# A graph layer with edge sums, a linear-attention mix and a 30-step feed-forward: W's products of two groups placed in the chain to the mix, and two VectorE pieces of the first stage placed earlier

## The chip, the cores and the metric

The kernel runs on one core of one Trainium2 chip. The metric is the device time of one execution in microseconds (us); the time before is 4202.76 us, the median of 4 runs (4201.67 to 4215.41). A profile is one further execution, with its own time. In the profile PE is TensorE's matmul, PEld its weight load, DVE is VectorE, ACT is ScalarE, POOL is GpSimd and SP is SyncE, which here issues DMAs.

## The reference

`x` has 12500 nodes of 256 features; there are 200000 edges (`src`, `dst`, `edge_weight`), sorted by `dst`. All is float32.

```python
xn = layernorm(x)
agg = segment_sum((xn @ W)[src] * edge_weight[:, None], dst)           # edges
q, k, v = (split_heads(xn @ w.T) for w in (wq, wk, wv))                # 4 heads of 64
k, v = layernorm(k) * gk + bk, layernorm(v) * gv + bv                  # per head
kv = einsum('sd,se->de', k, v) / N                                     # per head
x = x + relu(agg) + concat_heads(q @ kv) @ wo.T + bo
h = layernorm(x)
for _ in range(30):
    h = h + 0.01 * tanh(h); h = silu(h); h = layernorm(h) * lw + lb; h = h @ Wf.T + b
x = x + h
```

## The kernel before, in words

Nodes stand in 98 tiles of 128, in 25 groups of four tiles (the last has two). Instructions are issued in an order that is written out by hand (`manual_schedule`), and each engine runs its own in that order.

**First stage** (the loop at L574, one group of `x` per turn). `x` is loaded (L89), its statistics are taken on DVE (`stats_of_x`, L506 and L508) and raised to the power -1/2 on POOL (L510, L512), DVE makes the shift (L519), ACT normalizes (L529), SP stores the rows to `xnd` in DRAM (L91), PE transposes them (L541) and ACT copies them to `xnT` (L547). The edge lists (`dst`, `src`, `edge_weight`) are turned to columns beside that (L374 to L422). `wkv`, the matrix of keys and values, is centred over its rows at L491 to L497 and over each head at L607 to L611 (`hm`), the latter in turn g == 2. From g == 3 on each turn also makes the keys and values of one tile.

**Keys and values.** For each tile t PE multiplies `xnT` by `wkv` (L288), ACT squares (L295), DVE sums (L299), ACT takes the root (L301), DVE inverts and scales (L305, L306), and two tiles later PE adds the product of keys and values to `pacc` (L314, `kv_product`). The tiles from 24 on run in the loop at L793.

**Edges.** 128 edges are one gather: POOL issues an indirect DMA (L182) of 128 rows of `xnd` into one of 16 buffers `xg`. Four gathers are a quad and two quads an octet. DVE builds selection matrices (L208, L213, L221), PE multiplies a quad's rows by them (`sum_quad`, L234), ACT copies an octet's sum (`copy_quads`, L245), and PE adds it to a window of nodes in PSUM (`add_quads`, L259). When no later octet touches 64 nodes, ACT copies them to `aT`, the group's transposed sums, and DVE clears them (`free_nodes`, L273 and L274). A gather is issued only when the quad that used its buffer before has been summed: at most 16 gathers stand ahead of the sums (`gathers`, L179). In the loop at L793 `octet_at` says after which tiles an octet is summed; they are tiles 30, 33, 37, ..., 86, 90, 93 and 97.

**The chain to the mix** (L823 to L863). From `pacc` on, each product needs the one before: `psum_kv` (L824), times `lk` (L829), copied to `y` (L832), times `rv` (L836), scaled to the block-diagonal `bd` (L839), times `wq` (L847), copied and centred over rows (L849 to L852), times `wo` (L856), plus the bias to `mix` (L861). Between these stand five calls of `another_quad` (L830, L833, L840, L848, L860): what is due of an earlier octet, one quad's sum, four gathers. `p_kv`, three PSUM buffers, holds the products.

**Steps** (`plan`, L872, and the loop at L1024). A step is a "mix" of one group (`xnT` times `mix`, plus `x`, L1076), a "W" of one group (`aT` times `wg`, plus the rows of `accw`, which are zeros unless an edge fell outside the windows, then relu, added to `base`, L1080 and L1081), or one "pass" of the 30-step loop for one group: transposes (L998), copies (L1005), product (L1011), tanh (L957), DVE (L963), silu (L964), statistics (L970), power on POOL (L976), scaling (L984). All these products stand at L1011. `plan` lists the steps beforehand from assumed costs (3.5 us a matrix, 4.4 a pass, 1.25 a gather, a pass of the same group 14.0 later), with how many quads and gathers go with each step; it takes all gathers issued so far as landed. A group's passes start when its "mix" and "W" are done, and at most five groups are active.

Of the kernel before, what the change touches and what calls it, by code (L numbers as in the profile page):

```python
# [8 lines left out]
F32 = mybir.dt.float32  # L9
# [21 lines left out]
def gps_layer(  # L31
# [135 lines left out]
    class Edges:  # L167
# [4 lines left out]
        freed = 0  # L172
        xg, sel, selq, sq, aT = {}, {}, {}, {}, {}
# [147 lines left out]
    with ExitStack() as ph:  # L321
# [167 lines left out]


        for i, name in enumerate(("k", "v")):  # L491
            nat = w_nat[name]
            cm = small.tile([P, KC], F32, name="cm")
            nc.vector.tensor_reduce(cm, nat, AX.X, ALU.add)
            nc.vector.tensor_scalar(cm, cm, 1.0 / C, None, ALU.mult)
            nc.vector.tensor_tensor(nat, nat, cm[:, :, None].to_broadcast([P, KC, C]), ALU.subtract)
            nc.scalar.copy(wkv[:, :, i * C : (i + 1) * C], transposes_of(nat))  # L497

# [69 lines left out]


# [4 lines left out]
        for g in range(NG + 2):  # L574
# [10 lines left out]
            if g < NG:  # L585
                stats_of_x(g)
            if 0 <= g - 2 < NL:
                list_stored(g - 2)
# [17 lines left out]
            if g == 2:  # L606
                wh = wkv.rearrange("p k (h d) -> p (k h) d", d=D)  # L607
                hm = small.tile([P, KC * 2 * HEADS], F32, name="hm")
                nc.vector.tensor_reduce(hm, wh, AX.X, ALU.add)
                nc.vector.tensor_scalar(hm, hm, 1.0 / D, None, ALU.mult)  # L610
                nc.vector.tensor_tensor(wh, wh, hm[:, :, None].to_broadcast([P, KC * 2 * HEADS, D]), ALU.subtract)  # L611
# [101 lines left out]
    with ExitStack() as ph:  # L713
# [16 lines left out]
        gcol = w1.tile([D, 2], F32, name="gcol")  # L730
        wo_nat = w1.tile([P, KC, C], F32, name="wo_nat")
# [55 lines left out]
        for t in range(kv_done, NT + 2):  # L787
            octet_at[t] = spent > 12.5 + 10.3 * n
            n += octet_at[t]
            spent += 2.3 + (2.2 if octet_at[t] else 0.0)  # L790
# [23 lines left out]
        def another_quad():  # L814
            copy_quads()
            free_nodes()
            selections(1)
            add_quads()
            sum_quad()
            gathers(Q)  # L820


# [3 lines left out]
        nc.vector.memset(bd, 0.0)  # L826
        py = p_kv.tile([D + 1, HEADS, P], F32, name="pkv")
        for hd in range(HEADS):
            nc.tensor.matmul(py[:, hd, :], lhsT=psum_kv[:, hd, :], rhs=lk[:, hd % (P // D), :], start=True, stop=True)  # L829
        another_quad()  # L830
        y = w1.tile([D + 1, HEADS, P], F32, name="y")
        nc.vector.tensor_copy(y, py)  # L832
        another_quad()  # L833
        pbd = p_kv.tile([P, HEADS, D], F32, name="pkv")
        for hd in range(HEADS):
            nc.tensor.matmul(pbd[:, hd, :], lhsT=y[:, hd, :], rhs=rv, start=True, stop=True)  # L836
        for hd in range(HEADS):
            r = slice(hd % (P // D) * D, (hd % (P // D) + 1) * D)
            nc.vector.tensor_scalar(bd[r, hd // (P // D), r], pbd[r, hd, :], 1.0 / N, None, ALU.mult)  # L839
        another_quad()  # L840


# [5 lines left out]
        another_quad()  # L848
# [3 lines left out]
        nc.vector.tensor_tensor(at, at, am[:, :, None].to_broadcast([P, KC, C]), ALU.subtract)  # L852
        pm = p_kv.tile([P, KC, C], F32, name="pkv")
# [6 lines left out]
        another_quad()  # L860
# [11 lines left out]
    def plan():  # L872
# [151 lines left out]
    for k in range(K + 3):  # L1024
# [150 lines left out]
```

## Time and profile before

| | us |
|---|---|
| median of 4 runs | 4202.76 |
| the profiled execution | 4214.08 |
| its span | 4212.3 |
| PE busy / PEld busy | 4072.4 / 3388.9 |
| DVE / ACT / POOL busy | 3400.7 / 2526.8 / 2575.3 |
| first stage, tiles 24 to 97 | 0 to 124, 124 to 396 |
| chain to the mix, until `mix` is there | 397.7 to 424.2 |
| first "mix" step's product, first "pass" step's product | 425.65, 483.92 |
| last gather's slice, then passes alone | about 3500, to 4212.3 |

The profile's page gives busy times and the span in 40 slices; its timeline gives every instruction's start, duration, shape and, in brackets, the idle time before it and what ended that; a table by stretches gives busy time and the clock that PE was granted (1.00 is full). Matmuls of float32 are recorded as two each. Starts of matmuls are measured and their ends modelled.

### The profile page before, as it was taken

To read this page: it belongs to the slowest core of one execution; us is meant where nothing else is said; L and a number is where in the kernel's file an instruction comes from. 1 tells how busy PE (TensorE), PEld (TensorE's weight loads), DVE (VectorE), ACT (ScalarE), POOL (GpSimd) and SP (SyncE) were. 2 spreads that over 40 slices of the span, in tenths; PEclk is the share of its full clock that TensorE was granted. 3 is DMA by queue.
4 is the path that set the end of the run, shared out by engine and by line. 5 is a ranking of instruction groups with operands and counts; after the bars stand their busy time and mean duration, and the time that the engine had idled before them with its cause. 6 is when DMAs were issued, how large, how long until landed. Compare 5 with 4: busy or idle time off the path is not lost.

```text
span 4212.3 us, 68082 instructions
## 1 busy us (share of the span) xinstructions
PE 4072.4 (97%) x24201; PEld 3388.9 (80%) x24201; DVE 3400.7 (81%) x7389; ACT 2526.8 (60%) x3762; POOL 2575.3 (61%) x3186
## 2 busy tenths in 40 slices
PE   8797899999999999999999999999999999999999
PEld 4454678888888888888788888887888888788888
DVE  8454568888888888888888888888888888888887
ACT  7332245666665666666666666656666666677776
POOL 3466667777767777777677777666666662222222
PEclk9898999999999999999999999999999999999999
DMA  8333422222222222222222222122221210000000
GB/s 259 93 88 88 150 87 66 64 67 62 64 64 78 81 61 70 70 64 63 79 75 70 70 64 74 58 80 71 67 66 57 66 51 9 21 1 1 1 1 23
DMA packets 147687, 278.36 MB, mean 66 GB/s; under 512 B 28047, under 2 KB 97197, under 8 KB 147341
## 3 DMA queue, kind: packets, MB, share of 16 engines
q0 software_dynamic: 75024, 204.97, 16.5%
q1 hardware_dynamic: 72173, 68.42, 5.2%
q8 instruction: 197, 3.23, 0.3%
q14 instruction: 149, 1.22, 0.1%
q10 hardware_dynamic: 144, 0.52, 0.0%
HBM read 247.68 MB, written 26.12 MB: 65 GB/s over the span
## 4 chain that ended last, share of the span: by engine, by line
PE 79%; DVE 12%; ACT 4%; issue 3%; another core or an unknown queue 1%; POOL 1%; DMA 0%; DVEq 0%; POOLq 0%; ACTq 0%
PE po L1011 54%; PE pt L998 14%; PE pq L234 4%; PE pa L259 3%; DVE z L984 3%; PE pkv L288 2%; DVE st L970 2%; DVE s L963 2%; ACT s L957 2%; DVE v L299 1%; PE pacc L314 1%; DVE x_st L506 1%; POOL rs L976 1%; DVE f_st L1131 0%
## 5 line engine op out<-in xcount | busy, mean ns | idle before, releaser
L1011 PE MATMUL po<-w,zT 128*128 128x256 f32 x11760 | 2669.8, 380 | 4.5 <-DVE big L1070 2.1
L1011 PEld LDWEIGHTS po<-w,zT 128*128 128x128 f32 x11760 | 2178.8, 190 | 282.2 <-issue 11.1
L182 POOL DMA_INDIRECT xg<-xnd,src_i x1563 | 1596.1, 1021 | 505.2 <-issue 341.5
L963 DVE SCALAR_TENSOR_TENSOR s<-s,po 128x1024 f32<-128x1024 f32 (+1 forms) x725 | 864.9, 1193 | 356.6 <-ACT s L957 306.8
L984 DVE TENSOR_SCALAR z<-s,st,rs 128x256 f32<-128x256 f32 x2940 | 1042.6, 418 | 68.8 <-POOL rs L976 66.4
L964 ACT ACTIVATE s<-s 128x1024 f32<-128x1024 f32 (+1 forms) x750 | 780.5, 1041 | 489.7 <-DVE s L963 478.5
L970 DVE BATCH_NORM_STATS2 st<-s 128x6 f32<-128x512 f32 x1470 | 937.7, 679 | 115.6 <-ACT s L964 100.4
L957 ACT ACTIVATE s<-po 128x1024 f32<-128x1024 f32 (+1 forms) x725 | 730.2, 1007 | 243.9 <-PE po L1011 224.0
L1005 ACT ACTIVATE zT<-pt 128x512 f32<-128x512 f32 x1470 | 801.0, 602 | 65.8 <-PE pt L998 59.4
L998 PE MATMUL pt<-ident,z 128*128 128x128 f32 x5880 | 789.0, 276 | 36.4 <-DVE z L984 34.8
L998 PEld LDWEIGHTS pt<-ident,z 128*128 128x128 f32 x5880 | 671.9, 142 | 170.1 <-issue 76.4
L976 POOL TENSOR_TENSOR rs<-ve,mhalf 128x4 f32<-128x4 f32 (+1 forms) x750 | 764.7, 1020 | 62.5
L974 POOL TENSOR_SCALAR ve<-st 128x4 f32<-128x4 f32 (+1 forms) x750 | 146.3, 195 | 977.8 <-DVE st L970 938.1
L245 ACT COPY sq<-pq 128x256 f32<-128x256 f32 x196 | 72.3, 369 | 354.4 <-PE pq L234 248.4
L234 PE MATMUL pq<-xg,sel 128*32 128x256 f32 x3126 | 219.2, 388 | 4.6 <-issue 3.5
L259 PE MATMUL pa<-selq,sq 128*128 128x192 f32 (+2 forms) x1168 | 186.7, 297 | 35.7 <-ACT sq L245 19.8
L259 PEld LDWEIGHTS pa<-selq,sq 128*128 128x128 f32 x1168 | 173.1, 195 | 48.0 <-ACT sq L245 21.7
L288 PE MATMUL pkv<-wkv,big 128*128 128x512 f32 x392 | 202.3, 639 | 9.7 <-DVEq L622 4.8
L273 ACT COPY aT<-pa 128x128 f32<-128x128 f32 x196 | 51.4, 262 | 216.9 <-PE pa L259 151.6
L234 PEld LDWEIGHTS pq<-xg,sel 128*32 128x32 f32 x3126 | 83.7, 109 | 103.9 <-issue 68.2
L299 DVE TENSOR_REDUCE v<-sq 128x8 f32<-128x512 f32 x98 | 66.7, 681 | 104.7 <-ACT sq L295 91.7
L288 PEld LDWEIGHTS pkv<-wkv,big 128*128 128x128 f32 x392 | 71.2, 200 | 69.8 <-issue 60.0
(150 smaller groups left out, 1534.7 us busy)
## 6 DMA issues: line engine op xcount, KB each, us to landing
xg<-xnd,src_i POOLq DMA_INDIRECT x1563
xt<-in_x_dram SPq DMA_DIRECT2D x48, 512.0 KB
xnd<-xt SPq DMA_DIRECT2D x24, 512.0 KB
xt<-accw SPq DMA_DIRECT2D x24, 512.0 KB
out_dram<-big SPq DMA_DIRECT2D x24, 512.0 KB
xg<-in_dst_dram SPq DMA_DIRECT2D x6, 128.0 KB
xg<-in_src_dram SPq DMA_DIRECT2D x6, 128.0 KB
xg<-in_edge_weight_dram SPq DMA_DIRECT2D x6, 128.0 KB
```

The costliest lines, as they stand in the source:

```text
L182: nc.gpsimd.indirect_dma_start(out=ed.xg[t], out_offset=None, in_=xnd, in_offset=bass.IndirectOffsetOnAxis(ap=src_i[:, t : t + 1], axis=0),)
L234: nc.tensor.matmul(ed.pq[j * 2 * WIN : (j + 1) * 2 * WIN, :], lhsT=sel[:, j, :], rhs=ed.xg.pop(q * Q + j), start=(q % 2 == 0), stop=last, ...
L259: nc.tensor.matmul(pa[:, k, c : c + hi - lo], lhsT=sq[:rows, k * P : (k + 1) * P], rhs=selq[:rows, lo - n0 : hi - n0], start=False, stop=( ...
L957: nc.scalar.activation(flat(s, nt), flat(h, nt), AF.Tanh)
L963: nc.vector.scalar_tensor_tensor(sf, sf, 0.01, flat(h, nt), op0=ALU.mult, op1=ALU.add)
L964: nc.scalar.activation(sf, sf, AF.Silu)
L970: nc.vector.bn_stats(st[:, q, :], s[:, q].rearrange("p c j -> p (c j)"))
L976: nc.gpsimd.tensor_tensor(rs[:, :nt], ve[:, :nt], mhalf[:, :nt], ALU.pow)
L984: nc.vector.tensor_scalar(z[:, j, :], s[:, j // 2, :, j % 2], sv[:, j, 1:2], rs[:, j : j + 1], ALU.subtract, ALU.mult)
L998: nc.tensor.transpose(pt[:, i, k, :], z[:, 2 * q + i, k * P : (k + 1) * P], ident)
L1005: nc.scalar.activation(zT[:, 2 * q : 2 * q + 2], pt, AF.Copy, bias=1.0)
L1011: nc.tensor.matmul(po[:, j // 2, :, j % 2] if paired else po[:, j, :], lhsT=lhsT(j, k), rhs=rhs[:, k, :], start=(k == 0 and (j % 2 == 0 or ...
```

## The change

Four things. (1) `stats_of_x(0)` stands ahead of the centring of `wk` and `wv`, and the centring over heads (`hm`) stands in turn g == 1 instead of g == 2. (2) The `accw` rows of groups 0 and 1 are loaded to buffers of their own (`acs`, 512 KB each) before `wo`, `f_nat` and the small vectors, and the "W" products of groups 0 and 1 are made in the chain, in four halves through `p_kv`; DVE adds `accw` and writes the halves over `aT`. Their relu is added to `base` in the group's "mix" step. (3) No octet is summed in the last tiles: `octet_at` keeps tiles 30 to 86 and adds tile 98 (one turn after the last), and the chain sums two octets whole (`two_quads`) instead of five single quads. (4) `plan` starts with both "W" done.

```diff
-        for i, name in enumerate(("k", "v")):
-            nat = w_nat[name]
...
-            nc.scalar.copy(wkv[:, :, i * C : (i + 1) * C], transposes_of(nat))
...
+        stats_of_x(0)
+        for i, name in enumerate(("k", "v")):
+            nat = w_nat[name]
...
+            nc.scalar.copy(wkv[:, :, i * C : (i + 1) * C], transposes_of(nat))
+        wh = wkv.rearrange("p k (h d) -> p (k h) d", d=D)
+        hm = small.tile([P, KC * 2 * HEADS], F32, name="hm")
...
                 shift_of_x(g - 1)
             if g < NL:
                 list_values(g)
-            if g < NG:
+            if 0 < g < NG:
                 stats_of_x(g)
+            if g == 1:
+                nc.vector.tensor_reduce(hm, wh, AX.X, ALU.add)
+                nc.vector.tensor_scalar(hm, hm, 1.0 / D, None, ALU.mult)
+                nc.vector.tensor_tensor(wh, wh, hm[:, :, None].to_broadcast([P, KC * 2 * HEADS, D]), ALU.subtract)
             if 0 <= g - 2 < NL:
                 list_stored(g - 2)
             kv = None
...
-            if g == 2:
...
-                nc.vector.tensor_reduce(hm, wh, AX.X, ALU.add)
...
         lk = w1.tile([D + 1, P // D, P], F32, name="lk")
         rv = w1.tile([D + 1, D], F32, name="rv")
         gcol = w1.tile([D, 2], F32, name="gcol")
+        acs = [w1.tile([P, G, C], F32, name=f"ac{g}") for g in range(2)]
+        for g, (t0, nt) in enumerate(groups[:2]):
+            rows = accw[bass.ds(n_out * ((G + t0) * P), nt * P), :]
+            nc.sync.dma_start(out=acs[g], in_=rows.rearrange("(g p) c -> p g c", p=P))
         wo_nat = w1.tile([P, KC, C], F32, name="wo_nat")
         nc.sync.dma_start(out=wo_nat, in_=wo.rearrange("(k p) c -> p k c", p=P))
         f_nat = w1.tile([P, KC, C], F32, name="f_nat")
...
         octet_at, spent, n = {}, 0.0, 0
         for t in range(kv_done, NT + 2):
-            octet_at[t] = spent > 12.5 + 10.3 * n
+            octet_at[t] = t == NT or (t < NT - 9 and spent > 12.5 + 10.3 * n)
             n += octet_at[t]
             spent += 2.3 + (2.2 if octet_at[t] else 0.0)
         gathers(ROWS)
...
                 sum_quad()
                 gathers(O)
-        def another_quad():
-            copy_quads()
-            free_nodes()
-            selections(1)
-            add_quads()
-            sum_quad()
-            gathers(Q)
-
+        def two_quads():
+            for _ in range(2):
+                sum_quad()
+                gathers(Q)
+        halves_of = lambda g, h: ed.aT[g].rearrange("p k (g n) -> p g k n", n=P)[:, 2 * h : 2 * h + 2]
+        def w_product(g, h):
+            assert ed.freed >= (g + 1) * G * P // SLOT
+            pw = p_kv.tile([P, 2, C], F32, name="pkv")
+            for j in range(2):
+                for k in range(KC):
+                    nc.tensor.matmul(
+                        pw[:, j, :], lhsT=ed.aT[g][:, k, (2 * h + j) * P : (2 * h + j + 1) * P], rhs=wg[:, k, :],
+                        start=(k == 0), stop=(k == KC - 1),
+                    )
+            return pw
+        def w_stored(g, h, pw):
+            nc.vector.tensor_tensor(
+                halves_of(g, h), pw.rearrange("p g (k n) -> p g k n", n=P),
+                acs[g][:, 2 * h : 2 * h + 2].rearrange("p g (k n) -> p g k n", n=P), ALU.add,
+            )
+        selections(ed.summed + 4 - ed.selected)
         psum_kv = w1.tile([D + 1, HEADS, D + 1], F32, name="psum_kv")
         nc.vector.tensor_copy(psum_kv, pacc)
         bd = w1.tile([P, KC, P], F32, name="bd")
         nc.vector.memset(bd, 0.0)
+        two_quads()
         py = p_kv.tile([D + 1, HEADS, P], F32, name="pkv")
         for hd in range(HEADS):
             nc.tensor.matmul(py[:, hd, :], lhsT=psum_kv[:, hd, :], rhs=lk[:, hd % (P // D), :], start=True, stop=True)
-        another_quad()
         y = w1.tile([D + 1, HEADS, P], F32, name="y")
         nc.vector.tensor_copy(y, py)
-        another_quad()
+        copy_quads()
+        free_nodes()
+        pw = w_product(0, 0)
         pbd = p_kv.tile([P, HEADS, D], F32, name="pkv")
         for hd in range(HEADS):
             nc.tensor.matmul(pbd[:, hd, :], lhsT=y[:, hd, :], rhs=rv, start=True, stop=True)
+        w_stored(0, 0, pw)
         for hd in range(HEADS):
             r = slice(hd % (P // D) * D, (hd % (P // D) + 1) * D)
             nc.vector.tensor_scalar(bd[r, hd // (P // D), r], pbd[r, hd, :], 1.0 / N, None, ALU.mult)
-        another_quad()
+        pw = w_product(0, 1)
+        add_quads()
+        w_stored(0, 1, pw)
         at = w1.tile([P, KC, C], F32, name="at")
...
         pm = p_kv.tile([P, KC, C], F32, name="pkv")
         for h in range(KC):
             nc.tensor.matmul(pm[:, h, :], lhsT=bd[:, h, :], rhs=wq_n[:, h, :], start=True, stop=True)
-        another_quad()
         nc.vector.tensor_copy(at, pm)
         nc.vector.tensor_reduce(am, at, AX.X, ALU.add)
         nc.vector.tensor_scalar(am, am, 1.0 / C, None, ALU.mult)
         nc.vector.tensor_tensor(at, at, am[:, :, None].to_broadcast([P, KC, C]), ALU.subtract)
+        free_nodes()
+        for h in range(2):
+            w_stored(1, h, w_product(1, h))
+        ed.weighted = 2
         pm = p_kv.tile([P, KC, C], F32, name="pkv")
         for m in range(KC):
             for h in range(KC):
...
                     pm[:, m, :], lhsT=at[:, h, m * P : (m + 1) * P], rhs=woT[:, h, :],
                     start=(h == 0), stop=(h == KC - 1),
                 )
-        another_quad()
+        two_quads()
         nc.vector.scalar_tensor_tensor(
             mix, bo_r[:, None, :].to_broadcast([P, KC, C]), 1.0 / C, pm, op0=ALU.mult, op1=ALU.add
         )
...
             item, nq, cost, start = None, 0, 0.0, None
             octets = NO if quads == NQ else quads // 2
             while summed < len(groups) and octets > last_of[min((summed + 1) * G, NT) * P // SLOT - 1]:
-                whole.append(summed)
+                if summed >= ed.weighted:
+                    whole.append(summed)
                 summed += 1
             ready = [g for g, (last, it, at) in active.items() if last + APART <= k and at <= now + 1.0]
-            wanted = whole and mixed <= whole[0]
+            wanted = mixed < ed.weighted or (whole and mixed <= whole[0])
             if wanted or (not whole and not ready and mixed < len(groups)):
                 item, cost = ("mix", mixed), T_MATRIX
+                if mixed < ed.weighted:
+                    based[mixed] = k
                 mixed += 1
             elif whole:
                 item, cost = ("W", whole.pop(0)), T_MATRIX
...
         elif kind2 == "mix":
             nt = groups[g2][1]
             nc.vector.tensor_tensor(base[g2], pos.pop((kind2, g2))[:, :nt, :], xts.pop((kind2, g2))[:, :nt, :], ALU.add)
+            if g2 < ed.weighted:
+                aT = ed.aT.pop(g2).rearrange("p k (g n) -> p k g n", n=P)
+                for i in range(KC):
+                    bk = base[g2][:, :, i * P : (i + 1) * P]
+                    nc.vector.scalar_tensor_tensor(bk, aT[:, i], 0.0, bk, op0=ALU.max, op1=ALU.add)
         elif kind2 == "W":
             nt = groups[g2][1]
             ac = xts.pop((kind2, g2))[:, :nt, :]
```

More of the change, by code (lines that the diff above doesn't have):

```diff
@@ L172, in gps_layer @@
         freed = 0
+        weighted = 0
         xg, sel, selq, sq, aT = {}, {}, {}, {}, {}
@@ L487, in gps_layer @@
         nc.vector.memset(dmax, -1e9)
-        for i, name in enumerate(("k", "v")):
-            nat = w_nat[name]
[L493 to L496, printed above, removed]
-            nc.scalar.copy(wkv[:, :, i * C : (i + 1) * C], transposes_of(nat))
         norms, xns = {}, {}
@@ L567, in any_outside @@
             return flag_i
+        stats_of_x(0)
+        for i, name in enumerate(("k", "v")):
+            nat = w_nat[name]
+            cm = small.tile([P, KC], F32, name="cm")
+            nc.vector.tensor_reduce(cm, nat, AX.X, ALU.add)
+            nc.vector.tensor_scalar(cm, cm, 1.0 / C, None, ALU.mult)
+            nc.vector.tensor_tensor(nat, nat, cm[:, :, None].to_broadcast([P, KC, C]), ALU.subtract)
+            nc.scalar.copy(wkv[:, :, i * C : (i + 1) * C], transposes_of(nat))
+        wh = wkv.rearrange("p k (h d) -> p (k h) d", d=D)
+        hm = small.tile([P, KC * 2 * HEADS], F32, name="hm")
         NL = len(work)
@@ L605, in gps_layer @@
                 list_transposes(g - 1)
-            if g == 2:
[L607 to L611, printed above, removed]
             if kv:
```

## The prediction

> **What bounds the kernel now.** First the page's busy times and slices: PE is busy 97% of the span at nearly full clock, and only the first slices fall short.
>
> ```profile
> PE 4072.4 (97%) x24201; PEld 3388.9 (80%) x24201; DVE 3400.7 (81%) x7389; ACT 2526.8 (60%) x3762; POOL 2575.3 (61%) x3186
> ...
> PE   8797899999999999999999999999999999999999
> ```
>
> PE's work is the same in both kernels (the same products, elsewhere), so the change is worth what it takes from PE's idle and half-clock time. The table by stretches says where that lies (PE busy, PEld, DVE, ACT, POOL, granted clock, DMA share, GB/s):
>
> ```profile
> 394.00:404.00 10.00, 7.98 (x46) 6.13 (x47) 3.89 (x14) 0.33 (x2) 7.42 (x9) 0.50 0.32 96
> 404.00:410.00 6.00, 0.67 (x4) 0.48 (x3) 0.00 (x0) 0.25 (x1) 4.63 (x5) 0.50 0.37 109
> 410.00:415.00 5.00, 3.09 (x16) 1.98 (x16) 0.28 (x2) 0.32 (x2) 1.89 (x2) 0.50 0.26 79
> 415.00:424.50 9.50, 7.86 (x24) 5.18 (x24) 5.35 (x18) 0.44 (x2) 7.29 (x8) 0.50 0.31 89
> ...
> 500.00:560.00 60.00, 51.16 (x269) 40.43 (x268) 36.74 (x87) 20.95 (x32) 33.43 (x38) 0.92 0.33 97
> 560.00:600.00 40.00, 40.00 (x251) 33.85 (x250) 27.34 (x55) 18.26 (x29) 28.89 (x33) 1.00 0.37 109
> 600.00:650.00 50.00, 45.29 (x258) 36.34 (x257) 39.34 (x87) 27.30 (x40) 28.59 (x36) 1.00 0.22 69
> ```
>
> The chain (394 to 424.5) runs at half clock, and for 6 us nothing but POOL works. The timeline shows why:
>
> ```profile
> 402.70 1.97 PE L836 MATMUL pkv<-rv,y 65*128 65x64 f32 x8 [0.69 <-DVE y L832]
> ...
> 409.75 0.37 ACT L245 COPY sq<-pq 128x256 f32<-128x256 f32 x1 [13.37 <-remote]
> ...
> 411.41 0.95 POOL L182 DMA_INDIRECT xg<-xnd,src_i  x1 [0.30 <-issue]
> ...
> 414.71 0.95 DVE L839 TENSOR_SCALAR bd<-pkv 64x64 f32<-64x64 f32 x4 [11.40 <-PE pq L234]
> ...
> 415.08 0.94 POOL L182 DMA_INDIRECT xg<-xnd,src_i  x1 [2.73 <-remote]
> ```
>
> `bd` waits on L836, which ended at 404.67, yet starts at 414.71: 10.0 us late. ACT's copy is 7.7 late (its sum ended at 402.0). POOL had issued gathers without a pause since 392.0; everything resumes 2.3 us after the last of them ends (412.36). The same at each octet among the tiles:
>
> ```profile
> 376.04 1.30 PE L234 MATMUL pq<-xg,sel 128*32 128x256 f32 x16
> 377.19 0.95 POOL L182 DMA_INDIRECT xg<-xnd,src_i  x1 [0.30 <-issue]
> 379.88 0.60 ACT L295 ACTIVATE sq<-pkv 128x512 f32<-128x512 f32 x1 [4.01 <-PE pkv L288]
> 380.19 0.94 POOL L182 DMA_INDIRECT xg<-xnd,src_i  x1 [2.05 <-PE pkv L288]
> ```
>
> So I read: while gathers run back to back for over some 6 us, PE's "done" arrives late, by 1 to 5 us each and by more behind a quad's signals, until POOL pauses.
>
> **Part 1, the early statistics.**
>
> ```profile
> 19.07 1.20 DVE L609 TENSOR_REDUCE hm<-wkv 128x16 f32<-128x1024 f32 x1
> ...
> 20.63 1.22 DVE L611 TENSOR_TENSOR wkv<-wkv,hm 128x1024 f32<-128x1024 f32 x1
> ...
> 22.00 3.52 PE L288 MATMUL pkv<-wkv,big 128*128 128x512 f32 x4 [2.10 <-DVE x_sh L519]
> ```
>
> The three `hm` instructions hold DVE from 19.07 to 21.77, and the first L288 waits for them. After: statistics from 5.42 (1.68 us), the centring done at 10.4 instead of 8.8, ACT's second copy at 12.2, `hm` 12.4 to 15.2, list 0's extremes to 16.0, the shift at 16.03 as before. The next shift then needs only POOL's power (ends 19.33), and PE, through with L408 at 19.90, starts L288 at about 19.95: -2.0 us. POOL's two small instructions now precede list 0 and lie in its 6.62 us wait. From there turns take 3.98 to 4.35 us, set by DVE and ACT in lockstep, so the lead lasts. Bounds: 0, should `x` come late, and -2.3.
>
> **Part 2, the loads of `acs`.** Two SP issues (0.4 us each) and 1 MB, 7 us at the 145 GB/s of 125 to 150, ahead of `wo` and the others. Their first user is L753 at 159.56; `f_nat` is issued at 131.48, so 28 us cover it. The gathers share the DMA; the first octet is at 157.45, 14 us after its last gather was issued. Cost 0, at most 3.
>
> **Part 3, the last tiles.** At 365.99 before sums the octet of tile 90; after, tiles 91 to 97 go on without octets and, from 368 on, without gathers. One wait stays (tile 89's late signal, 1.5 us). Seven tiles at 2.24 (the spacing of L288 between octets), pacc and one octet (1.07): the octet of turn 98 ends at **385.3**. Before had ended its own at 392.1, having summed two octets more.
>
> **Part 4, the chain**, with full-clock rows (L829, L836, L847, L856 at half of 1.97, 1.97, 2.08, 3.78; half a "W" 1.81, half of L1011's 3.62; storing it 0.69, as L306). POOL starts 16 gathers at 385.6 and ends at 405.6, so signals are late from about 391.5 to 408. DVE makes four selections (2.3 us) before `psum_kv` at 389.0; L829 ends 390.1, the first half "W" 391.9 (beside `y`), L836 393.0. Its signal takes 2.3 us (mean of those I read), then `bd` 0.95; the second half and one addition fill PE to 395.6. L847 ends about 397.5 to 399, signal and centring (2.3 + 2.3) until 402 to 403.5, PE meanwhile on group 1 (3.6). L856, `two_quads` and `mix` follow by 407 to 410. The halves stored ahead of `bd` and `at` add 0.7 each there.
>
> Then gathers bound: the next octet's rows land at 408.1 (POOL's end plus 2.5, as at 391.54, which had waited for the gather of 388.97). First "mix": 409.5 to 415. The octet after that was issued only after `two_quads`: 8 x 1.25 + 2.5 later, 418.5 to 423; PE waits some 5 us. The second "mix" ends between 423 and 428. By then before's list up to 450.04 is done except two octets (1.07 + 0.85 each, L234 and L259): 427 to 432 against 450.0. **Parts 3 and 4: -18 to -23**, taken as -20. A low clock is the upper end.
>
> The clock's row: it fell to 0.50 at 394, with no PE gap before it over 0.8 us, so I let the chain run partly at half. The Trainium skill ("TensorE: Matmul & The Clock Gate", "What's actually happening") has the clock halved after an idle window of some 3.4 us; by that the waits here of under 3 us would leave it full and the sum would stand at its lower end, -23.
>
> **Part 5, the steps.** `plan` is arithmetic; starting from 40 quads and 176 gathers (before: 45 and 196) it gives 798 steps for 800, the third, fourth and fifth group starting at steps 15, 39 and 67 (before: 12, 31, 59), more "mix" steps between, and the same last 144 steps. It takes 16 gathers as landed that are not, and POOL stays behind by 20 gathers (25 us), so late signals go on as in 500 to 560, where PE is busy 51.16 of 60. Eight steps more with three groups, 5.3 us each at the 9% that 600 to 650 loses, are +4; bounds -1 and +9. Two loads of `accw` less at SP, and the same DVE work (two 1.22 before; four 0.69 and four of 0.69 after, +1.1 hidden, since DVE is busy 28 of 50 there): 0.
>
> **Sum:** -2 - 20 + 4 = **-18 us**: the profiled execution from 4214.1 to 4196, and the median, 11.3 below it, from 4202.8 to 4185.
>
> **Rivals.** (A) Gathers starve PE: if it waits for all 25 us that POOL owes, the gain is eaten, 4203 +- 5. For: PE waits for gathers twice in part 4. Against: POOL is busy 61%, and "mix" steps fill. (B) The two late signals of the chain both wait until POOL stops, and later stretches lose the upper bound: -10, 4193. For: the 10 us at L839. (C) Slower: with three groups too few to cover a pass (19 to 28 us from one product to the next of the same group, in the timeline), PE runs at 85% as in 500 to 560 over steps 22 to 66, some 230 us: +34 against -22, 4215 or more. It decides when PE falls below 90% there. Against: 560 to 600 is 100% busy with three groups. (D) The change doing less than it says: in the built order of PE the W halves stand where written, so only part 1 could be without effect: 4187, inside the forecast.
>
> **How the numbers follow.** A measurement tells 0.3%, 12.6 us: 4190.2 and 4215.4 are the marks. Forecast 0.62 (4174 to 4190), B 0.17 and A 0.12 (mostly within 0.3%), C 0.09. A fast half of B counts as faster. Faster 0.66, within 0.27, slower 0.07. The range leaves out C and the slow half of A and takes in the bounds (-23 - 2 - 1 gives 4177, with 4 us for the loose signals 4173): 4173 to 4201.
>
> **What would show it.** Right: L288 first at about 20; no ACT wait over 2 us in tiles 92 to 97; `mix` 18 to 21 us after `psum_kv` (26.5 before: 397.7 to 424.2); L839 no more than 5 us behind L836; first pass some 20 us sooner than 483.92. Wrong: L839 again 10 us late; PE below 85% after 450; the two waits for gathers longer than 7 us.

## The result, and the profile after

The changed kernel takes 4201.8 us in the median of 42 runs (4193.99 to 4208.63), the kernel before 4205.07 of 63 (4194.48 to 4219.09): a ratio of 0.9991, 95% interval 0.9986 to 0.9995, or 3.8 us. Forecast were 18. The profiled execution took 4200.63 us, its span is 4198.8. The page of after, its busy times and the slices of PE:

```profile
PE 4065.9 (97%) x24201; PEld 3379.6 (80%) x24201; DVE 3401.4 (81%) x7393; ACT 2525.5 (60%) x3762; POOL 2574.1 (61%) x3186
...
PE   8798899999999999999999999999999999999999
```

PE does the same work and is about as busy as before. The table by stretches of after, columns as before (PE busy, PEld, DVE, ACT, POOL, granted clock, DMA share, GB/s):

```profile
394.00:404.00 10.00, 5.46 (x17) 4.26 (x16) 2.54 (x7) 0.27 (x1) 3.19 (x4) 0.67 0.20 62
404.00:410.00 6.00, 6.00 (x24) 4.94 (x22) 3.53 (x7) 0.00 (x0) 0.00 (x0) 0.81 0.00 0
...
424.50:432.00 7.50, 4.08 (x9) 1.90 (x8) 0.00 (x0) 0.00 (x0) 4.73 (x5) 0.65 0.35 104
...
500.00:560.00 60.00, 57.62 (x338) 46.16 (x339) 42.96 (x96) 28.22 (x43) 39.19 (x45) 1.00 0.34 101
560.00:600.00 40.00, 37.88 (x222) 29.99 (x223) 27.50 (x56) 18.34 (x27) 25.99 (x32) 1.00 0.30 87
600.00:650.00 50.00, 47.05 (x276) 38.84 (x268) 38.44 (x83) 26.86 (x39) 32.88 (x39) 1.00 0.30 91
```

The first steps with three groups, rival C's ground, are better filled than before (57.62 of 60 against 51.16). But half-clock and empty time is still there from 394 to 432. The timeline of after (start, duration, engine, line) says why. L857 and L865 are the former L829 and L836, L869 is L839; L836 is now the "W" product, and L843 adds `accw` to a half of it:

```profile
381.97 1.09 PE L857 MATMUL pkv<-lk,psum_kv 65*65 65x128 f32 x8 [0.44 <-DVE psum_kv L851]
...
382.90 1.89 PE L836 MATMUL pkv<-wg,aT 128*128 128x256 f32 x8
...
386.93 0.37 ACT L246 COPY sq<-pq 128x256 f32<-128x256 f32 x1 [7.83 <-remote]
...
390.50 0.69 DVE L859 COPY y<-pkv 65x512 f32<-65x512 f32 x1 [8.31 <-remote]
...
391.24 1.97 PE L865 MATMUL pkv<-rv,y 65*128 65x64 f32 x8 [6.45 <-issue]
...
397.15 0.95 POOL L183 DMA_INDIRECT xg<-xnd,src_i  x1 [0.30 <-issue]
400.32 0.69 DVE L843 TENSOR_TENSOR aT<-pkv,ac 128x512 f32<-128x512 f32 x1 [8.95 <-remote]
401.10 0.95 DVE L869 TENSOR_SCALAR bd<-pkv 64x64 f32<-64x64 f32 x4
...
410.27 0.69 DVE L896 SCALAR_TENSOR_TENSOR mix<-bo_r,pkv 128x512 f32<-128x512 f32 x1 [1.03 <-PE pkv L891]
```

L857 ends at 383.06 and its reader `y` starts at 390.50, 7.4 us late. L865 ends at 393.21 and its reader `bd` starts at 401.10, 7.9 late. Between them DVE waits for the first half of "W", which ended at 384.79: its addition starts at 400.32, 15.5 us late and 2.2 us after POOL's last gather of the run ends (398.10). POOL had issued gathers every 1.25 us since 378.40. The trace also records each update of PE's semaphore: those of L857, of the first half and of L865 came at 390.47, 400.30 and 401.07, in PE's order, and the readers started within 0.03 us of them. So it is the signal that is late. `y` got its own while the gathers still ran, the other two only behind them. So the chain has two long waits for its own products where before had one, and takes 28.8 us from the start of `psum_kv` to that of `mix` (25.8 before). A second place is the second "mix" product:

```profile
424.50 0.38 PE L1049 MATMUL po<-mix,big 128*128 128x256 f32 x1 [0.78 <-issue]
...
427.33 1.98 PE L1049 MATMUL po<-mix,big 128*128 128x256 f32 x3 [1.42 <-issue]
...
430.83 1.44 PE L1049 MATMUL po<-mix,big 128*128 128x256 f32 x3 [1.52 <-issue]
...
434.09 0.37 ACT L246 COPY sq<-pq 128x256 f32<-128x256 f32 x1 [15.32 <-remote]
```

PE takes from 424.5 to 436.6 for a product that elsewhere lasts 3.6 us, in pieces, while the third batch of gathers runs; ACT reads an octet's sum some 10 us after it is done (last L235 slice ends 423.73). Before these pieces PE waits for nothing that the profile shows ("issue"), so what held it there stays open.

### The profile page after: what moved, and what is told of

It reads as the page before. It is cut to its first block, busy times and chain, and to the rows that moved or that the text cites. A ratio compares the mean times of both kernels' runs of the same rounds, so it can differ in the third digit from the quotient of the medians.

```text
span 4198.8 us, 68080 instructions
## 1 busy us (share of the span) xinstructions
PE 4065.9 (97%) x24201; PEld 3379.6 (80%) x24201; DVE 3401.4 (81%) x7393; ACT 2525.5 (60%) x3762; POOL 2574.1 (61%) x3186
## 3 DMA queue, kind: packets, MB, share of 16 engines
q14 instruction: 150, 1.22, 0.1%
## 4 chain that ended last, share of the span: by engine, by line
PE 76%; DVE 12%; issue 3%; ACT 3%; POOL 1%; another core or an unknown queue 1%; POOLq 0%; DVEq 0%; ACTq 0%
PE po L1049 52%; PE pt L1036 13%; PE pq L235 4%; DVE z L1022 4%; PE pa L260 3%; DVE st L1008 3%; PE pkv L289 3%; DVE s L1001 2%; ACT s L995 2%; POOL rs L1014 1%; PE pacc L315 1%; ACT s L1002 1%; DVE f_st L1174 0%; DVE big L1108 0%
## 5 line engine op out<-in xcount | busy, mean ns | idle before, releaser
L1043 ACT ACTIVATE zT<-pt 128x512 f32<-128x512 f32 x1470 | 801.7, 602 | 64.4 <-PE pt L1036 53.1
L246 ACT COPY sq<-pq 128x256 f32<-128x256 f32 x196 | 72.4, 369 | 324.4 <-PE pq L235 245.8
L235 PE MATMUL pq<-xg,sel 128*32 128x256 f32 x3126 | 216.8, 385 | 6.0 <-issue 5.9
L235 PEld LDWEIGHTS pq<-xg,sel 128*32 128x32 f32 x3126 | 83.1, 109 | 103.1 <-issue 62.0
```

The source lines that it names most:

```text
L235: nc.tensor.matmul(ed.pq[j * 2 * WIN : (j + 1) * 2 * WIN, :], lhsT=sel[:, j, :], rhs=ed.xg.pop(q * Q + j), start=(q % 2 == 0), stop=last, ...
L1043: nc.scalar.activation(zT[:, 2 * q : 2 * q + 2], pt, AF.Copy, bias=1.0)
```

## The experiments

Two measures are used. The **stages** of a profile: the start of `psum_kv`, from there to the start of `mix` (the prediction's 18 to 21 counted to its end, 0.7 more), the first "pass" product. And the **loss of the steps**: from the point where PE has done 600 us of work (each product at its spacing at full rate: 0.216 us a record of L1011, 0.109 a transpose, 0.075 one of L234) to where it has done 3850, the time that went by less the 3250 of work. That stretch begins at 751 to 777 us in the first table and ends before 4100.

The runs fell on two kinds of chip. On one the kernel before takes 4204 to 4205 us, on the other 4118 to 4119. Ratios are always to the kernel before on the same chip. First the chips with 4204, profiles of one execution each:

```
kernel (profile)          psum_kv  to mix  first pass  loss of steps   ratio to before (95%)
before                    397.7    25.8    483.9       64.5
before, again             394.9    24.1    484.4       63.9
before, head              393.8    25.8    483.1       -
part 1 alone              390.4    24.1    473.2       64.4            0.9994 (0.9979 to 1.0009)
changed                   381.5    28.8    471.8       73.5            0.9991 (0.9986 to 0.9995)
changed, again            384.1    27.0    474.1       74.4            0.9989 (0.9979 to 0.9999)
changed, head             384.4    28.5    474.4       -
fewer gathers by order    381.2    26.1    456.0       72.9            1.0001 (0.9990 to 1.0012)
held until mix            389.8    12.6    449.7       75.7            0.9971 (0.9959 to 0.9983)
octets as before          400.7    28.0    501.9       64.5            0.9999 (0.9989 to 1.0009)
```

Then those with 4119:

```
changed, third            330.8    12.6    396.7       69.7            0.9970 (0.9958 to 0.9982)
held until mix            330.1    12.6    383.2       66.6            0.9970 (0.9958 to 0.9982)
held until bd             329.0    12.6    382.0       66.9            0.9969 (0.9957 to 0.9981)
quads in two turns        335.1    12.6    401.0       67.2            0.9980 (0.9971 to 0.9989)
octets as before          333.9    15.2    403.9       60.9            0.9958 (0.9944 to 0.9971)
both of these             338.9    13.7    405.0       62.7            0.9964 (0.9951 to 0.9978)
held until bd, two turns  334.1    12.6    387.2       66.3            0.9982 (0.9973 to 0.9991)
held until bd, octets as before  335.1  15.1  390.4    65.5            0.9950 (0.9937 to 0.9964)
```

**The heads alone.** Both kernels cut behind the same set of steps, 17 of the changed one (shown) and 19 of the one before, which has two "W" more:

```diff
-    steps = plan()
+    steps = plan()[:17]
...
+    for g, (t0, nt) in enumerate(groups):
+        rows_io(out, base[g], t0, nt, False, nc.sync)
```

> The kernel before, cut after its first 19 steps (13 mix, 3 W, 3 passes), with all 25 groups' rows written out at the end; the rest of the steps is left out. To be set against the changed kernel cut at the same set of steps (17 steps, two W being in the chain). Theory 1 (the gain is made in the head in every execution and lost later): the two heads' medians differ by 20 to 28 us, as the two profiles do at this step (507.2 against 531.7, 24.6). Theory 2 (the one profile of before showed a head about 10 us slower than usual, as its whole time was 9 above its median): the medians differ by 10 to 16 us, and the new profile of this head reaches the product of the first mix step some 10 us sooner than 425.65.

> The changed kernel cut after its first 17 steps, with the same rows written out at the end; the rest of the steps is left out. Theory 1: median 20 to 28 us under that of the head of before, and its profile again has the scaling of bd 7 us behind its product and the second mix step stretched from 418 to 437 while 16 gathers run back to back. Theory 2: median 10 to 16 us under it, with the same timeline.

Medians 565.87 us (six runs, 552.58 to 571.48) and 558.51 (546.51 to 564.79): 7.4 apart, under what either theory named, with a scatter of 19 us for one kernel. Only one run of the first and two of the second lie within 1.5% of the lowest, so the medians are loose; lowest against lowest is 6.1. The changed head has also summed three octets less. So the head varies from run to run as the whole kernel does (4194 to 4219), and the two profiles of before lie 9 and 7 us above its median. The 7.4 are too few runs to weigh a few us; what they show is that the 24.6 between the first two profiles was not the usual distance.

**Part 1 alone.**

> The kernel before with part 1 of the change alone (first statistics of x ahead of the centring, head means in turn 1). The trace of the changed kernel is 2.5 us ahead from the first product of keys and values on, and 4.4 from 138 us on. Theory 1 (a lead in the head lasts where nothing later absorbs it): 2 to 4.5 us under before, and a lead of 2.5 in its trace at 50 us. Rival: the gathers, which are bound by POOL's pace from 135 us on, set the tiles' times, and the lead is gone by 400 us: 0 to -1 us.

The first L288 starts at 19.25 instead of 22.00, 2.8 us sooner, and `psum_kv` some 5 sooner than in the mean of before's three. The ratio can't tell 2.5 us from nothing. The profile is of a quick execution (4196.92 us, the median is 4201.95), so its first pass at 473.2, as soon as the changed kernel's, is not the usual one. Its list of steps is that of before, and its loss is 64.4: three profiles with this list agree within 0.6 us, which makes the loss a sharp measure.

**Gathers out of the chain, by order.**

```diff
-                gathers(O)
+                if t < NT:
+                    gathers(O)
...
-                gathers(Q)
...
-        two_quads()
```

> The changed kernel without any gather from turn 98 until mix is there: 16 gathers are issued in the steps instead, and the second octet of the chain is summed there too; everything is still computed. Theory of late signals (back-to-back gathers delay PE's signals by 7 us twice in the chain): no wait over 3 us behind a finished product, 16 to 18 us from psum_kv to mix instead of 28.8, and mix at about 398 instead of 411. If the steps then make up for the 16 gathers beside their other work, the whole is 5 to 12 us under the changed kernel; if the gathers that are owed hold the steps, it comes out within 4 us of it. Rival (the chain is long because of the halved clock and the order of PE, not of the gathers): 25 us or more from psum_kv to mix, with waits of 5 us or more behind finished products.

This held nothing back: POOL ran ahead of the chain and issued 11 of the steps' gathers in it, from 378 to 391, since nothing but free buffers holds it. `y` still came 11 us late, and the chain took 26.1 us. But the second half of the chain, without gathers, had no late signal, and the first pass came 16 us sooner than in the changed kernel. Nothing of it was left at the end (1.0001).

**Gathers held until `mix`.** As before, and POOL now waits:

```diff
+        held = w1.tile([1, 1], F32, name="held")
+        nc.gpsimd.tensor_copy(held, mix[:1, 0, :1])
```

> As the run without gathers from turn 98 on, but POOL now reads one element of mix ahead of the 24 gathers that follow, so that none can be issued before mix is there (in the former run POOL ran ahead and issued 11 of the steps' gathers in the chain). All is computed. Theory of late signals: no wait over 2 us behind a finished product in the chain, and psum_kv to mix in 12 to 15 us (28.8 in the changed kernel, 26.1 with 11 gathers). Rival (clock and order of PE): 20 us or more. For the whole: the steps start with 24 gathers fewer, and their list has 174 passes that come four steps after the same group's last (143 in the changed kernel, 115 before); theory that the steps give back what the head wins: within 6 us of the changed kernel, with 8 to 14 us more lost after 700 us. Rival (the head's time goes through to the end): 12 to 16 us under the changed kernel.

> The changed kernel with gathers held until mix is there, again. Where the kernel before takes about 4119, it was 12.5 under it, and there 3 to 8 us over the changed kernel, since nothing is late that it could mend, and its steps begin with 24 gathers fewer. On a chip with late signals: psum_kv to mix in 12 to 16 us instead of 28.8, and the whole within 6 us of the changed kernel.

On the chip with 4204 the timeline and the table by stretches of this run:

```profile
389.78 0.42 DVE L851 COPY psum_kv<-pacc 65x260 f32<-65x260 f32 x1
...
391.38 0.69 DVE L859 COPY y<-pkv 65x512 f32<-65x512 f32 x1 [0.91 <-PE pkv L857]
...
393.95 0.95 DVE L869 TENSOR_SCALAR bd<-pkv 64x64 f32<-64x64 f32 x4
...
402.42 0.69 DVE L895 SCALAR_TENSOR_TENSOR mix<-bo_r,pkv 128x512 f32<-128x512 f32 x1 [1.03 <-PE pkv L891]
...
403.33 0.18 POOL L899 COPY held<-mix 1x1 f32<-1x1 f32 x1 [36.91 <-issue]
```

```profile
390.00:403.00 13.00, 12.13 (x64) 10.64 (x64) 7.85 (x18) 0.76 (x3) 0.00 (x0) 1.00 0.00 0
```

No gather, no late signal: 12.6 us from `psum_kv` to `mix`, PE busy 12.13 of 13 us, full clock. With the same products in the same order up to L891 this was 27 to 28.8 in the changed kernel, and on the second kind of chip, with the gathers, it is 12.6 again. That shows the cause of the long chain: gathers beside it, on the first kind of chip. It is one profile there. By the ratios the whole is 12.2 us under before and 7.6 under the changed kernel on the same chip: more than "within 6 us", less than the rival's 12 to 16, although its steps lose most (75.7). With 4119 it neither gains on the changed kernel nor loses the 3 to 8 us expected (both 0.9970): the changed chain takes 12.6 us there too.

**An octet's quads in two turns**, four gathers released at a time instead of eight:

```diff
-            if octet_at[t]:
-                sum_quad()
-                sum_quad()
-                gathers(O)
+            for _ in range(2 if t == NT else int(octet_at[t] or (t < NT and octet_at.get(t - 1, False)))):
+                sum_quad()
+                gathers(Q)
```

> The changed kernel with an octet's two quads summed in two turns of the tiles (turn t and t + 1) instead of one, so that four gathers (5 us) are released at a time instead of eight (10 us). Same plan. Theory of late signals (PE's signals are late only while gathers run back to back for over some 6 us): no ACT wait of over 1.5 us behind L289 or L235 in the tiles from 36 on, and the last octet of the tiles 5 to 15 us sooner; the whole 3 to 12 us under the changed kernel. Rival (the pace of POOL, 8 x 1.25 of each 12.2 us, sets the tiles, and signals are late whatever the burst): tiles within 3 us, the whole within 3 us.

This run and its combinations fell only on chips with 4119, where no signal was late: 0.9980, with the tiles 4 us longer, so there the 3 to 12 us under the changed kernel did not come. Whether shorter runs of gathers keep the signals in time on the other chips is not tried.

**Octets as before**, at tiles 90, 93 and 97, none in turn 98:

```diff
-            octet_at[t] = t == NT or (t < NT - 9 and spent > 12.5 + 10.3 * n)
+            octet_at[t] = spent > 12.5 + 10.3 * n
```

> The changed kernel with the octets at tiles 90, 93 and 97 as before and none in turn 98; the chain with W's products stays, and the plan starts from 44 quads and 192 gathers instead of 40 and 176. Its list starts the third, fourth and fifth group at steps 11, 32, 61 (changed kernel: 15, 39, 67; before: 12, 31, 59), and has 129 passes four steps after the same group's last from step 90 on (143; 115). Theory that deferred octets cost later: the tiles end 4 to 8 us later than in the changed kernel, and the steps after 700 us lose 3 to 6 us less (67 to 70 against 73.5; before 64.5); the whole within 4 us of it. Rival (the losses of the steps do not depend on the list): 73 lost after 700 us and the whole 3 to 6 us over the changed kernel.

> Both of the former: octets as before to tile 97, each summed in two turns. Theory of late signals and of deferred octets together: the fastest of the four, 5 to 15 us under the changed kernel, with a loss after 700 us of 67 to 70. Rivals: same as those of the two parts, then within 4 us of the changed kernel.

> The changed kernel with the octets at tiles 90, 93 and 97 as before, again: it was the fastest on the chip where the kernel before takes 4119, 17.9 under it. There: 16 to 20 under before, and 2 to 6 under the changed kernel of the same call. On a chip with late signals: within 5 us of the changed kernel.

The loss of the steps falls by 9 to 10 us on both kinds of chip: 74.4 to 64.5, and 69.7 to 60.9, more than expected. With 4204 the tiles and the chain take all of it back (`psum_kv` 17 us later, first pass 28 later, ratio 0.9999). With 4119 the tiles lose only 3 us, and the kernel is 17.9 us under before (4101.17 against 4119.06). With two turns as well it is slower (4104.35), not the fastest. Against the changed kernel the two ratios lie on opposite sides on the two kinds (0.9999 to 0.9989, 0.9958 to 0.9970), but their intervals overlap.

**The changed kernel and the kernel before, again.**

> The changed kernel itself once more, with the kernel before on the same chip. The four runs before this one fell on a chip on which the kernel before takes 4119 us (4204 on the chip of the runs ahead of them), and on which no signal of PE came late in the tiles although POOL issued gathers without a pause. Theory (the late signals ate the head's gain, and they are a matter of the chip): where the kernel before takes about 4119, the changed one is 12 to 20 us under it, about as forecast; where it takes about 4204, 0 to 8 us under it, as measured. Rival (the gain is small because of the steps' list, on every chip): 0 to 8 us under it on either chip.

> The kernel before, for a profile on this chip. Where it takes about 4119: no PE wait over 3 us behind POOL from 160 to 390, L839 of the chain within 2 us behind its product, and a loss after 700 us of 64 to 65, as in the two profiles with the same list. Where it takes about 4204: the chain again some 26 us from psum_kv to mix, and a first mix step within 8 us of 425.

> The changed kernel again. Where the kernel before takes about 4119 us (signals on time), theory: 12 to 20 us under it; rival (steps' list): 0 to 8. Where it takes about 4204: 0 to 8 under it, and a third profile of it for the stages (psum_kv at 383 +- 2, mix 27 to 29 us later, 73 to 75 lost after 700 us).

With 4204: 0.9989, as the first result, and in the kernel before 24.1 us from `psum_kv` to `mix`. With 4119: 10.7 us under before by the medians (4107.80 against 4118.47), 12.4 by the ratio (the interval allows 7 to 17): by the medians between the two theories, by the ratio just inside the first. How that divides between head and steps stays open, as no profile of the kernel before was taken on such a chip. There the chain runs as forecast, but the first "mix" product does not follow `mix` at 343.4; table by stretches and timeline of that run:

```profile
331.00:344.00 13.00, 12.73 (x76) 11.06 (x80) 7.86 (x18) 0.77 (x3) 9.88 (x11) 1.00 0.37 106
344.00:353.00 9.00, 5.05 (x34) 2.35 (x27) 2.28 (x11) 0.80 (x3) 6.63 (x8) 0.88 0.68 219
```

```profile
343.33 1.07 PE L235 MATMUL pq<-xg,sel 128*32 128x256 f32 x16
...
346.06 1.05 PE L235 MATMUL pq<-xg,sel 128*32 128x256 f32 x10
...
350.07 0.62 PE L235 MATMUL pq<-xg,sel 128*32 128x256 f32 x2 [2.96 <-DMA xg<-xnd,src_i]
...
352.41 3.94 PE L1049 MATMUL po<-mix,big 128*128 128x256 f32 x13
```

Two octets stand in PE's order between L891 and that product. The first (343.33) has its rows; the second (346.06), which the steps sum, waits for its gathers: 9 us from `mix` to its first use, 4 of them empty. In the held versions neither stands there, and the product follows `mix` by 0.8.

**Held until `bd` only**, alone, with two turns, and with the octets as before: the copy reads `bd[:1, 0, :1]` and stands behind L869.

> As the run that held the gathers until mix is there, but held only until bd is scaled, 8 us sooner there (394.4 against 402.4). The rest of the chain has three signals of PE to wait for in these 8 us, and signals came late only after some 6 us of gathers. Theory: psum_kv to mix in 12.5 to 15 us all the same, and the gathers 7 us ahead, so 1 to 6 us under that run where signals come late (which was 8.9 under the changed kernel). Rival (any gather delays signals): 17 to 22 us from psum_kv to mix, and the whole 0 to 6 us over that run.

> Gathers held until bd, and an octet's two quads summed in two turns of the tiles, so that POOL gets four gathers at a time instead of eight. Theory of late signals after 6 us of gathers: where the kernel before takes about 4204, the tiles end 5 to 15 us sooner than with eight at a time (psum_kv at 370 to 380 instead of 384), and most of it stays. Rival (signals are late by POOL's share of the time, whatever the burst): psum_kv at 382 to 390, the whole within 3 us of the run with gathers held until bd. On a chip with signals on time the spread costs nothing or up to 4 us.

> Gathers held until bd, and the octets at tiles 90, 93 and 97 as before (none in turn 98): the plan starts from 42 quads and 168 gathers instead of 38 and 152, and its list has 146 passes four steps after the same group's last instead of 174. Theory: the steps after 700 us lose 66 to 72 instead of 75.7, the tiles end 8 to 14 us later, the whole within 5 us of the run with gathers held until bd. Rival (the steps' list decides): 6 or more under it.

> Gathers held until bd, octets as before, again: the fastest where signals are on time (20 us under before). There again 17 to 22 under before. Where the kernel before takes about 4204, theory (the chain's late signals are mended, the octets at 90, 93 and 97 cost the tiles 8 to 14 us there, the steps' list gives some 6 back): psum_kv to mix in 12.5 to 15 us, the whole 6 to 16 under before. Rival (octets in the tiles are dear where signals are late, as the version with octets as before showed, 0.9999): within 5 us of before.

> Gathers held until bd, four at a time in the tiles, again (7 us under before where signals are on time, that is 5 over the version with eight at a time). Where the kernel before takes about 4204, theory of a limit of some 6 us: psum_kv at 370 to 380 and psum_kv to mix in 12.5 to 15, the whole 12 to 25 under before. Rival (signals late by POOL's share of the time): psum_kv at 382 to 390, the whole 5 to 12 under before.

All five fell on chips with 4119, so what they were to tell of late signals stays open. Held until `bd` (0.9969) is as good as held until `mix` (0.9970); with two turns it is 0.9982 both times. With the octets as before it is the fastest version of the study: 4098.39 and 4099.16 us, 20 under before, ratios 0.9950 and 0.9953 (0.9940 to 0.9967). Its loss is 65.5 with 146 passes four steps after the last of their group, where on such chips the list with 129 lost 60.9, that with 143 lost 69.7 and that with 174 lost 66.6: the count does not order the losses.

**Where the steps lose.** The table by stretches of after, then of before, at three stretches where old groups end and new ones begin:

```profile
1000.00:1300.00 300.00, 293.39 (x1801) 249.06 (x1800) 253.93 (x554) 187.01 (x272) 212.68 (x253) 1.00 0.23 67
...
1950.00:2150.00 200.00, 190.87 (x1159) 160.63 (x1152) 167.88 (x380) 119.85 (x176) 138.59 (x165) 1.00 0.26 77
...
3450.00:3720.00 270.00, 256.66 (x1385) 220.67 (x1385) 224.82 (x464) 174.75 (x241) 72.69 (x121) 0.99 0.04 12
```

```profile
1000.00:1300.00 300.00, 296.25 (x1820) 252.50 (x1816) 253.81 (x555) 185.12 (x269) 216.53 (x255) 1.00 0.23 68
...
1950.00:2150.00 200.00, 193.75 (x1173) 162.31 (x1172) 171.00 (x393) 123.17 (x182) 142.35 (x165) 1.00 0.26 79
...
3450.00:3720.00 270.00, 259.12 (x1415) 224.25 (x1413) 227.81 (x471) 177.82 (x245) 75.48 (x122) 0.99 0.04 14
```

PE does 2.5 to 2.9 us less in each (1300 to 1950 gives 3.0 back, in part because after stands some 20 us further in its list; another 3 us or so of the loss falls at 750 to 800). The changed list has fewer other steps to put between passes there: 21 of 25 "mix" steps stand in its first 50, 17 in before's, because the third, fourth and fifth group start later. The octets put back take the 9 to 10 us away, but they change two things together, the list and the 16 gathers and four quads that the steps start with, and no run parts them. That it is the missing "mix" steps is only argued: the list of the held kernel has 24 of the 25 in its first 50, and with 4119 it lost 66.6, less than the changed kernel's 69.7.

## Why the prediction was wrong

The time forecast was 4185, the range 4173 to 4201, and it is 4201.8: of the 18 us forecast some 4 came.

- **Part 1**: forecast -2.0 at the first L288, measured -2.8 (22.00 to 19.23). Right, half a us past its bound of -2.3.
- **Part 2**: forecast 0. The lead of 4.5 us at the first gather (124.53 to 120.03) is 4.4 at the first octet (157.45 to 153.00). Right.
- **Part 3**: seven tiles at 2.24 came so (L288 at 365.40, 367.64, 369.88), and `psum_kv` starts at 381.5 to 384.4, sooner than the 389.0 forecast; before has 393.8 to 397.7. In the means of three that is 12 us, part 1 included, for the 9 and 2 forecast. Right.
- **Part 4**, the step that failed: "Its signal takes 2.3 us (mean of those I read)". That was the price of L865's signal (L836 there), which took 7.9. L857's signal (L829 there) stood in the sum at nothing, `y` being made beside the first half "W"; it took 7.4. A third, L879's, was also put at 2.3 and came on time, the gathers having stopped. The mechanism was named, late signals while gathers run back to back; its size was wrong. The 2.3 was a mean over many signals, while the same signal in the profile of before, the 10.0 us at L839, was left to rival B. The reading "for over some 6 us" failed too: the sum that ended at 381.53 reached ACT at 386.93, 5.4 us late, and the first update of its slices that was over a us late came at 382.60, 4.2 us after the first gather started. The chain takes 27 to 29 us instead of 17 to 20, no less than before's 24 to 26; `bd` starts 7.9 us behind its product where 5 was the sign of being right. Rival B had both waits long, at -10; that both last until POOL stops holds for the second alone.
- **The wait for gathers** behind `mix` was forecast at some 5 us and the second "mix" to end by 423 to 428. It ends at 436.6, while the third batch of gathers runs. With the two octets still owed (3.8 us) that is 10 us ahead of before's 450.0, for the 18 to 23 forecast.
- **Part 5**: forecast +4, bounds -1 to +9; the loss of the steps went from 64 to 74, +10 and just past the upper bound. The reason given, three groups in the first 60 steps, was not where it fell: those stretches are fuller than before. Most of it fell where groups change, from 1000 us on. The +1.1 of DVE work beside it does not follow from its terms either: eight of 0.69 are 5.5 us, against 2.4 or, with two of 1.22 for each group, 4.9; DVE had room for it.
- **From profile to median**: the sum carried the distance of 11.3 us between the profile of before and its median over to the changed kernel. It is no constant. By the heads' runs, which scatter by 19 us, it lies in the head; the first profile of the changed kernel lies 1.2 us under its median, the second 4 over it. The profile that was read had more to lose than the usual run.

By the medians: 3.8 us gained and 10 lost in the steps leave some 14 of head for the 22 forecast, an estimate. Against the profile that was read, the head was nearly as forecast: where PE has done 600 us of work, after is 22 and 15 us ahead of it. In part that is luck. By the second "mix" the lead was 10 us, and the stretch from 500 to 560, where PE is busy 57.62 instead of 51.16, gave 6.5 more, for which the prediction had no term.

The clock row is where a rule was weighed. Behind its 6.45 us wait L865 takes 1.97 us, twice the 1.00 of the held run, and the clock from 394 to 404 is 0.67. In the held run, with no wait over 1 us in the chain, it is 1.00. These two runs agree with the Trainium skill ("TensorE: Matmul & The Clock Gate", "What's actually happening"), which halves the clock after an idle window of some 3.4 us. The full clock that the prediction weighed by that rule hung on waits under 3 us, and the waits were longer. The kernel before is not explained so: its clock fell to 0.50 at 394 with no gap of PE over 0.8 us ahead of it, and no run here shows why.

## What to carry to other kernels

A queue that runs ahead was held only by data here: with its instructions moved behind the chain in the program 11 gathers still ran inside it, and one small read of the awaited result took the chain from 27 us to 12.6. Work that is put off is priced where it lands, in the list that a planner makes of it, and not by what it saves where it stood. And a forecast of less than 1% from one profile needs a second profile of the same kernel first: the distance to the median lay in the very stage that was to be changed.

## What the runs showed of the hardware

The late signals were seen on some chips and not on others. The kernel with octets as before, the same stage of the tiles, first where before takes 4204, then where it takes 4119; L235 sums an octet, L246 copies it:

```profile
275.85 1.07 PE L235 MATMUL pq<-xg,sel 128*32 128x256 f32 x16
...
279.64 0.60 ACT L296 ACTIVATE sq<-pkv 128x512 f32<-128x512 f32 x1 [4.03 <-PE pkv L289]
279.95 0.94 POOL L183 DMA_INDIRECT xg<-xnd,src_i  x1 [2.02 <-PE pkv L289]
...
281.20 0.35 ACT L246 COPY sq<-pq 128x256 f32<-128x256 f32 x1
```

```profile
279.67 1.07 PE L235 MATMUL pq<-xg,sel 128*32 128x256 f32 x16
...
280.73 0.94 POOL L183 DMA_INDIRECT xg<-xnd,src_i  x1 [0.30 <-PE pq L235]
280.92 0.35 ACT L246 COPY sq<-pq 128x256 f32<-128x256 f32 x1
```

ACT starts the copy 4.3 us after the sum ends on the one and 0.2 on the other. Over 160 to 380 us this is 2.7 to 3.3 us in the mean and up to 12 in ten profiles on the first kind, and 0.6 at most in the mean, never over 0.9, in ten on the second (three chips), where POOL issues gathers for over 100 us with pauses of 0.3 in seven of the ten and for some 50 in the others. A gather takes POOL 0.95 us, 1.25 from start to start, on both. The kernel before takes 85 us, 2.0%, more on the first kind. Where that lies the changed kernel's profiles show (before has none on the second kind): `psum_kv` starts 51 to 54 us later there, the chain takes 14 to 16 longer and the first pass comes 75 to 78 later, of 94 to 96 us in its medians; behind 600 us of work the loss differs by 4 to 5. So nearly all of it lies ahead of that point, in the stages whose signals are late. That the late signals alone make it is likely but not shown, and what differs in the chips no run shows.
